# Number biases in Exp and Square, and one full-width product for both float16 halves, in a four-layer graph network

## The chip, the cores and the metric

The kernel runs on one NeuronCore of a Trainium2 chip. The metric is the device time of one execution in microseconds; the time of the kernel before is the median of three runs. The core's engines are named as in the profile: PE (TensorE, matrix products; PEld is its weight load), DVE (VectorE), ACT (ScalarE), POOL (GpSimd) and SP (SyncE, which issues most transfers).

## The reference

Four graph layers work on 4096 nodes with 64 features and one dense 4096 x 4096 adjacency matrix of zeros and ones. After every layer the input is added and a layer norm over the features follows.

```python
# layer 0: mean over neighbours, a linear map, relu, rows scaled to length one
h = (adj @ x + x) / clip(sum(adj, 1) + 1, 1); z = relu(concat([x, h]) @ W + b); z / norm(z)
# layers 1 and 3: attention in hyperbolic space, over all pairs (i, j)
adj_att = sigmoid(left[:, None] + right[None, :] + b_att) * adj
support = einsum('ij,ijd->id', adj_att, logmap(x[:, None], x[None, :]))
proj(expmap(x, support))
# layer 2: the last 100 neighbours of each node, weighted by powers of two
rank = cumsum(adj != 0, axis=1); deg = rank[:, -1:]; k = minimum(deg, 100)
w = mask * where(rank - (deg - k) > 0, 0.5 ** (deg - rank), 0)
w @ (x @ weight) + bias
```

In layer 2 an edge that is the n-th from the end of its row weighs 2 to the power of -n. The weight thus follows from a count of the edges that come after it.

## The kernel before, in words

Nodes are cut in 32 blocks of 128 (the neighbours j, on the partitions) and in four groups of 1024 (the nodes i, along the free axis). Each layer walks the groups in the order 3, 2, 1, 0 (`GROUPS`) and, within a group, the blocks from the last to the first. The adjacency matrix is read anew by every layer, in loads of two blocks by 1024 nodes (1 MB, `load`, six buffers); its values are taken as bfloat16 by reading every other 16-bit word. A check on DVE (`check`, L838) makes sure that the entries are zero or one. Work on rows (layer norm, the preparation of the next layer, turning of sums) is written as generators that wait in two queues; `tick`, called after every block or so, lets them go on. So row work is strewn between the blocks. In layers 0 and 2 the order of PE and ACT is the order of the program (`manual_schedule(engines=FIXED)`); DVE and POOL there, and all engines in layers 1 and 3, are ordered by the scheduler of the framework.

**Layers 1 and 3** (`attend`). For each block of 128 by 1024 pairs, PE makes scores in a PSUM tile `z` (L1059, L1062, L1065: six products of 512 columns), ACT takes a Sigmoid (L1074, bias is a column of `right`) and a Square of the scores (L1077, bias is the column `turn`, which holds one constant), DVE multiplies (L1080), and for two blocks at once adds and multiplies (L1082); PE sums into `acc` (L1037).

**Layer 2.** `count` (L1569) keeps, for each block, the number of later edges in a PSUM tile `z`. It is updated in place from block to block by two products of 512 columns for each 512 nodes: `pass_by` adds the edges of the block that has just been left, `enter` those of the new one. `weights_of` (L1576) makes the weights with an Exp whose bias is the column `at_edge`, which also holds one constant. The rows to be summed are kept as two float16 halves, high and low, side by side in `halves` (128 columns for each block). `add_up` (L1581) sums with four products of 64 columns: high and low half, each for the first and the second 512 nodes, into the two partition halves of one tile `acc`. All four lag one block behind the Exp.

Groups 3 and 2 go together (`wide_pass`, Exp of 1024 columns), then group 1 and group 0 one at a time (`narrow_pass`, Exp of 512 columns). The text calls these the two-group pass and the one-group passes. PSUM holds three tiles `z` of two banks. In layer 2 the third, `third_z`, gives its first half to the sums of the second group of the two-group pass and lends its second half to row work (`of_third`, in turn with `aux`).

At the end of a pass ACT copies the sums to SBUF (L1611), and `end_2` has PE turn them back to rows by four transposes (`to_rows_of`, L1095); DVE scales them and adds the bias (L1494, L1498), and layer norm and `prepare` follow: casts of `y` (L899 to L901), transposes (L943), copies of the turned rows (L947), and two small Ln (L950, L951).

Of the kernel before, what the change touches and what calls it, by code (L numbers as in the profile page):

```python
# [19 lines left out]
P = 128  # L20
N = 4096
D = 64
# [36 lines left out]
def gnn_stack_kernel(  # L59
# [509 lines left out]
    def stream(fits):  # L569

        with ExitStack() as st:
# [208 lines left out]

            two_i = keep.tile([P, P], BF16, name="two_i")
            V.tensor_scalar(two_i, ident, 2.0 * UNIT, None, ALU.mult)
            turn = num(keep, "turn", 1)
            V.memset(turn, ROOT + OFF)


            centre = keep.tile([P, 2, D + 1], F32, name="centre")
# [237 lines left out]
            def attend(layer, s, rate, then):  # L1025

                left_b = left_bs[s]

                acc = ps.tile([P, W], F32, name="acc")
                lag = []  # L1030

                def add_up(g, t, behind=None):

                    for k in (1, 0):
                        j = 2 * g + k
                        for h in range(2):
                            it = nc.tensor.matmul(  # L1037
                                acc[h * D : (h + 1) * D, :], xe[:, j, :],
                                t[:, k, h * W : (h + 1) * W],
                                start=j == BLOCKS[0], stop=j == BLOCKS[-1],  # L1040
                            )
                            if behind is not None:
                                in_order(it.ins, behind.ins)

                for g in reversed(range(NB // 2)):
                    _, edge = load(s, g)
                    need((layer, 2 * g // WB))
                    if g == 4 and then is not None:
                        later(in_turn((layer, then, "left"), spread_left(then)), True)
                    for k in (1, 0):  # L1050
                        j = 2 * g + k
                        of = slice(j * P, (j + 1) * P)

                        zp = z_tile()
                        for h in range(2):
                            half = zp[:, h * W : (h + 1) * W]
                            to = slice(s * WW + h * W, s * WW + (h + 1) * W)
                            at = k * WW + h * W
                            nc.tensor.matmul(  # L1059
                                half, two_i, edge[:, at : at + W], start=True, stop=False  # L1060
                            )
                            nc.tensor.matmul(  # L1062
                                half, hi_lo[:, of], lo_hi[:, to], start=False, stop=False
                            )
                            last = nc.tensor.matmul(  # L1065
                                half, src[:, of], dst[:, to], start=False, stop=True
                            )
                        if k == 1:
                            if len(lag) == 2:
                                add_up(*lag.pop(0), last)  # L1070
                            sq = sb.tile([P, 2, WW], F32, name="sq")
                            t = sb.tile([P, 2, WW], F32, name="t", bufs=3)
                        sig = sb.tile([P, WW], F32, name="sig", bufs=3)
                        nc.scalar.activation(  # L1074
                            sig, left_b, AF.Sigmoid, bias=right[:, j : j + 1]
                        )
                        nc.scalar.activation(  # L1077
                            sq[:, k], zp, AF.Square, bias=turn, scale=-1.0 / UNIT
                        )
                        V.scalar_tensor_tensor(t[:, k], zp, 0.0, sig, ALU.max, ALU.mult)  # L1080
                        tick(rate)
                    V.scalar_tensor_tensor(t, sq, HIGH**2, t, ALU.add, ALU.mult)  # L1082
                    lag.append((g, t))
                    tick(rate)
                for args in lag:
                    add_up(*args)
                sums = row.tile([P, W], F32, name="sums", bufs=2)
                nc.scalar.copy(sums, acc)
                return sums
# [200 lines left out]
            )  # L1290
            V.tensor_sub(enter, enter, edge_of)
            V.tensor_sub(pass_by, pass_by, enter)
            at_edge = num(keep, "at_edge", 1)
            V.memset(at_edge, -(OFF_EDGE + CUT) * LN2)


            w2_twice = keep.tile([P, D], F32, name="w2_twice")
            w2_hl = keep.tile([P, 2, D], F16, name="w2_hl")

# [188 lines left out]
            def end_2(s, sums):  # L1488
                z = grp("z0")
                yield 1  # L1490
                yield from free()
                t = to_rows_of(sums)
                yield 1
                V.scalar_tensor_tensor(  # L1494
                    z.rearrange("p (h k) f -> p h k f", h=2)[:, 0], t[:, 0], 2.0**CUT / SUP,
                    b2_sb[:, None, :].to_broadcast([P, SB, D]), ALU.mult, ALU.add,
                )
                V.scalar_tensor_tensor(  # L1498
                    z.rearrange("p (h k) f -> p h k f", h=2)[:, 1], t[:, 1], 2.0**CUT / SUP,
                    b2_sb[:, None, :].to_broadcast([P, SB, D]), ALU.mult, ALU.add,  # L1500
                )
                held.pop()
                yield 1
                V.tensor_add(z, z, x_of(2)[:, blocks(s), :])
                yield 1
                yield from norm_rows(3, s, z, x2[:, blocks(s)])
                yield from prepare(3, s, att3, batt3_sb, curve3, 1e-30, good[:, 1], 40)

            def wide_pass(two):

                zs = [z_tile() for _ in two]

                accs = [ps.tile([P, W], F32, name="acc"), third_z[:, :W]]
                behind, lag = [None, None], []
                for g in reversed(range(NB // 2)):
                    edges = [load_2(s, g) for s in two]
                    need((2, 2 * g // WB))
                    for k in (1, 0):
                        j = 2 * g + k
                        w = sb.tile([P, 2, WW], F32, name="sq").bitcast(BF16)[:, :, :WW]  # L1520
                        for i, edge in enumerate(edges):
                            here = edge[:, k * WW : (k + 1) * WW]
                            count(zs[i], behind[i], here, j, WW)
                            behind[i] = here
                            weights_of(zs[i], WW, w[:, i])
                            if i == 1:
                                for of, acc in enumerate(accs if lag else ()):
                                    add_up(acc, *lag[of])
                                lag = [(j, w[:, n, :W], w[:, n, W:]) for n in range(2)]
                            if two[0] != GROUPS[0] or j < BLOCKS[4]:  # L1530
                                tick(1)
                for of, acc in enumerate(accs):
                    add_up(acc, *lag[of])
                return accs

            def narrow_pass(s):

                zs = [z_tile() for _ in range(2)]
                acc = ps.tile([P, W], F32, name="acc")
                behind, lag = [None, None], []  # L1540
                for g in reversed(range(NB // 2)):
                    edge = load_2(s, g)
                    for k in (1, 0):
                        j = 2 * g + k
                        w = sb.tile([P, 2, WW], F32, name="sq").bitcast(BF16)[:, 0, :WW]
                        for h in range(2):
                            here = edge[:, k * WW + h * W : k * WW + (h + 1) * W]
                            count(zs[h], behind[h], here, j, W)
                            behind[h] = here
                            weights_of(zs[h], W, w[:, h * W : (h + 1) * W])  # L1550
                        if lag:
                            add_up(acc, *lag.pop(0))
                        lag.append((j, w[:, :W], w[:, W:]))
                        tick(1)
                add_up(acc, *lag.pop(0))
                return [acc]

            def load_2(s, g):
                a, edge = load(s, g)
# [13 lines left out]

            def weights_of(z, n, w):

                weighed[0] = nc.scalar.activation(w, z[:, :n], AF.Exp, bias=at_edge, scale=-LN2)  # L1576

            def add_up(acc, j, *ws):
                for part in range(2):
# [24 lines left out]
            with tc.manual_schedule(engines=FIXED):  # L1604
                spare.append(of_third)

                for some in (GROUPS[:2], GROUPS[2:3], GROUPS[3:]):
                    accs = wide_pass(some) if len(some) == 2 else narrow_pass(some[0])
                    for s, acc in zip(some, accs):
                        sums = row.tile([P, W], F32, name="sums", bufs=2)  # L1610
                        nc.scalar.copy(sums, acc)  # L1611
                        later(end_2(s, sums))
                spare_ends()

# [96 lines left out]
```

## Time and profile before

| | before |
|---|---|
| median of three runs | 1103.39 us (1102.56 to 1103.76) |
| the profiled execution | 1103.6 us |
| its span in the profile | 1101.8 us, mean granted TensorE clock 0.966 |
| PE busy | 997.7 us (91%) |
| DVE busy | 916.4 us (83%) |
| ACT busy | 795.1 us (72%) |
| layer 0, about | 0 to 195 us |
| layer 1, about | 195 to 520 us |
| layer 2, two-group pass | 520 to 629 us |
| layer 2, one-group passes | 629 to 750 us |
| layer 3 and the end | 750 to 1102 us |

The stage borders are read from the first and last starts of the lines named above. A share of busy time is a mean over stages of different kinds; what sets the time of a stage is seen in its own windows and timeline. A matmul's duration in the timeline is longer than the distance between the starts of two that follow each other, since they are pipelined: the distance is what counts.

### The profile page before, as it was taken

The page shows a single profiled execution, that of the slowest core. Times are in us where ns is not written, and L with a number is a line of the kernel's source. Part 1 is how long each engine was busy: PE and PEld are TensorE (multiplying, and loading weights), DVE is VectorE, ACT ScalarE, POOL GpSimd, SP SyncE. Part 2 cuts the span into 40 slices and gives each one's busy share as a digit, 9 for nine tenths or more (in the row PEclk, how much of TensorE's full clock was granted, in tenths as well). Part 3 has the DMA queues.
Part 4 walks back from the last instruction along what each step waited for, and adds up shares of the span by engine and source line. Part 5 has one row for each costly group of instructions (what it writes and reads, how often), then busy time and mean ns, then how long its engine had stood idle before and what let it go on. Part 6 is the DMA issues. An engine that isn't in the chain of part 4 may idle for free.

```text
span 1101.8 us, 13740 instructions
## 1 busy us (share of the span) xinstructions
PE 997.7 (91%) x4862; PEld 394.3 (36%) x4949; DVE 916.4 (83%) x1452; ACT 795.1 (72%) x886; POOL 273.5 (25%) x649
## 2 busy tenths in 40 slices
PE   4998997889999999998998998998899999999980
PEld 2454454333333333332333333322333333333320
DVE  6677976999999999999457395636999999999986
ACT  0003122979999999897676778989899999998950
POOL 0011210010053533625500010100001544346172
PEclk8999998889999999999998999999999999999995
DMA  9999999536666566655787988776556666666400
GB/s 358 378 411 388 369 421 382 189 122 223 214 244 211 195 234 214 222 198 184 271 304 280 366 298 277 273 261 229 191 192 217 241 228 202 238 222 228 163 1 23
DMA packets 38581, 271.63 MB, mean 247 GB/s; under 512 B 4710, under 2 KB 4710, under 8 KB 5734
## 3 DMA queue, kind: packets, MB, share of 16 engines
q1 hardware_dynamic: 37728, 270.03, 67.4%
q8 instruction: 41, 0.67, 0.2%
q10 hardware_dynamic: 774, 0.63, 0.2%
q14 instruction: 38, 0.31, 0.1%
HBM read 269.58 MB, written 1.05 MB: 246 GB/s over the span
## 4 chain that ended last, share of the span: by engine, by line
PE 56%; DVE 26%; ACT 8%; DMA 3%; POOL 3%; issue 3%; ACTq 0%; SPq 0%; POOLq 0%; DVEq 0%
PE acc L1037 15%; PE z L1569 9%; DVE t L1082 8%; PE z L1062 7%; PE z L1059 7%; PE z L1065 6%; DVE t L1080 6%; PE acc L1581 3%; PE acc L1414 3%; ACT sq L1077 3%; DMA edges<-in_adj_dram 3%; DVE junk L838 2%; ACT sq L1576 2%; PE z L1581 1%; POOL sq L869 1%
## 5 line engine op out<-in xcount | busy, mean ns | idle before, releaser
L1080 DVE SCALAR_TENSOR_TENSOR t<-z,sig 128x1024 f32<-128x1024 f32 x256 | 309.3, 1219 | 13.8 <-ACT sq L1077 7.5
L1077 ACT ACTIVATE sq<-z,turn 128x1024 f32<-128x1024 f32 x256 | 277.9, 1111 | 46.5 <-PE z L1065 19.4
L1082 DVE SCALAR_TENSOR_TENSOR t<-sq,t 128x2048 f32<-128x2048 f32 x128 | 297.4, 2324 | 0.5
L1074 ACT ACTIVATE sig<-left_b,right 128x1024 f32<-128x1024 f32 x256 | 286.0, 1146 | 1.9 <-DVE t L1080 1.3
L1037 PE MATMUL acc<-t,xe 128*64 128x512 f32 x1024 | 258.2, 614 | 16.5 <-DVE t L1082 15.7
L1062 PE MATMUL z<-lo_hi,hi_lo 128*128 128x512 f16 x512 | 195.4, 382 | 3.6 <-issue 0.7
L1065 PE MATMUL z<-dst,src 74*128 74x512 f16 x512 | 196.6, 384 | 0.0
L1059 PE MATMUL z<-edges,two_i 128*128 128x512 bf16 x463 | 183.0, 395 | 6.8 <-DVE t L1080 6.8
L1576 ACT ACTIVATE sq<-z,at_edge 128x512 bf16<-128x512 f32 (+1 forms) x192 | 149.2, 828 | 45.2 <-PE z L1569 41.9
L1037 PEld LDWEIGHTS acc<-t,xe 128*64 128x64 f32 x1024 | 64.3, 137 | 145.6 <-issue 85.1
L838 DVE SCALAR_TENSOR_TENSOR t<-edges 128x2048 bf16<-128x2048 f32 x32 | 73.0, 2288 | 37.0 <-DMA edges<-in_adj_dram 37.0
L1059 PEld LDWEIGHTS <-two_i 128*128 128x128 bf16 x512 | 50.5, 99 | 132.7 <-issue 83.9
L1569 PE MATMUL z<-edges,pass_by 128*128 128x512 bf16 x241 | 86.2, 395 | 11.0 <-ACT sq L1576 10.3
L1414 PE MATMUL acc<-edges,first 128*128 128x512 bf16 x241 | 77.0, 396 | 18.4 <-DMA edges<-in_adj_dram 17.9
L1569 PE MATMUL z<-edges,enter 128*128 128x512 bf16 x240 | 84.0, 393 | 0.5
L1414 PE MATMUL acc<-edges,third 128*65 128x512 bf16 x256 | 80.1, 394 | 0.8 <-issue 0.2
L838 DVE SCALAR_TENSOR_TENSOR junk<-edges 128x2048 bf16<-128x2048 f32 x32 | 73.2, 2286 | 4.8 <-DMA edges<-in_adj_dram 4.6
L1065 PEld LDWEIGHTS <-src 74*128 74x128 f16 x512 | 49.4, 97 | 71.0 <-issue 9.1
L1062 PEld LDWEIGHTS <-hi_lo 128*128 128x128 f16 x512 | 50.6, 99 | 54.9 <-issue 10.0
L1581 PE MATMUL acc<-sq,halves 128*64 128x512 bf16 x384 | 61.0, 395 | 2.4 <-issue 1.4
L869 POOL TENSOR_TENSOR sq<-z 128x512 f32<-128x512 f32 x8 | 14.2, 1777 | 166.5 <-DVE z L868 135.1
L1133 POOL TENSOR_TENSOR w_att<-x,u 128x512 f32<-128x512 f32 x6 | 15.6, 2596 | 142.1 <-ACT u L1128 142.1
(375 smaller groups left out, 938.4 us busy)
## 6 DMA issues: line engine op xcount, KB each, us to landing
edges<-in_adj_dram SPq DMA_DIRECT2D x256, 1024.0 KB, 4.9
x<-in_x_dram SPq DMA_DIRECT2D x4, 256.0 KB
out_dram<-x ACTq DMA_DIRECT2D x2, 256.0 KB
out_dram<-x SPq DMA_DIRECT2D x2, 256.0 KB
w_sb<-in_L_gnn_W_dram ACTq DMA_DIRECT2D x1, 32.0 KB, 5.4
w_twice<-in_L_gnn_weight_dram ACTq DMA_DIRECT2D x2, 16.0 KB, 7.4
given<-in_L_gnn_b_dram ACTq DMA_DIRECT2D x1, 0.2 KB
given<-in_L_gnn_bias_dram ACTq DMA_DIRECT2D x1, 0.2 KB
```

The lines of the kernel that those rows point to most:

```text
L838: V.scalar_tensor_tensor(junk, a, 0.0, a, ALU.not_equal, ALU.not_equal, accum_out=odd[:, n : n + 1])
L1037: it = nc.tensor.matmul(acc[h * D : (h + 1) * D, :], xe[:, j, :], t[:, k, h * W : (h + 1) * W], start=j == BLOCKS[0], stop=j == BLOCKS[-1],)
L1059: nc.tensor.matmul(half, two_i, edge[:, at : at + W], start=True, stop=False)
L1062: nc.tensor.matmul(half, hi_lo[:, of], lo_hi[:, to], start=False, stop=False)
L1065: last = nc.tensor.matmul(half, src[:, of], dst[:, to], start=False, stop=True)
L1074: nc.scalar.activation(sig, left_b, AF.Sigmoid, bias=right[:, j : j + 1])
L1077: nc.scalar.activation(sq[:, k], zp, AF.Square, bias=turn, scale=-1.0 / UNIT)
L1080: V.scalar_tensor_tensor(t[:, k], zp, 0.0, sig, ALU.max, ALU.mult)
L1082: V.scalar_tensor_tensor(t, sq, HIGH**2, t, ALU.add, ALU.mult)
L1414: nc.tensor.matmul(accs[h][:m], lhs[:, j, :], edge[:, at : at + W], start=j == BLOCKS[0], stop=j == BLOCKS[-1],)
L1569: nc.tensor.matmul(z[:, h : h + W], lhs, rhs[:, h : h + W], start=j == BLOCKS[0], stop=True, skip_group_check=True,)
L1576: weighed[0] = nc.scalar.activation(w, z[:, :n], AF.Exp, bias=at_edge, scale=-LN2)
```

## The change

The two constant columns `turn` and `at_edge` are gone; Square and Exp get the constants as numbers in the instruction. In the one-group passes the two halves of `halves` are no longer summed apart. One product with all 128 columns is made for each 512 nodes, so that the partitions of a sum hold the high half above and the low half below. There are now two tiles of sums, one for each 512 nodes: `acc` and the first half of `third_z`. Each product comes right behind the counting products of its own 512 nodes and takes the weights of the block before. After the pass both tiles are copied, and the two partition halves are added while the rows are turned back: eight float32 products with `stack`, two identity matrices of 64 above each other. The two-group pass sums as before.

```diff
-            turn = num(keep, "turn", 1)
-            V.memset(turn, ROOT + OFF)
...
-                            sq[:, k], zp, AF.Square, bias=turn, scale=-1.0 / UNIT
+                            sq[:, k], zp, AF.Square, bias=ROOT + OFF, scale=-1.0 / UNIT
...
-            at_edge = num(keep, "at_edge", 1)
-            V.memset(at_edge, -(OFF_EDGE + CUT) * LN2)
+            stack = keep.tile([P, D], F32, name="stack")
+            V.tensor_add(stack, ident[:, :D], ident[:, D:])
...
-                t = to_rows_of(sums)
+                if len(sums) == 1:
+                    t = to_rows_of(sums[0])
+                else:
+                    t = take(F32, P, SB, 2, D)
+                    for k in range(SB):
+                        for h, of in enumerate(sums):
+                            nc.tensor.matmul(
+                                t[:, k, h], of[:, k * P : (k + 1) * P], stack,
+                                start=True, stop=True,
+                            )
+                    t = t.rearrange("p k h f -> p h k f")
...
             def narrow_pass(s):
 
                 zs = [z_tile() for _ in range(2)]
-                acc = ps.tile([P, W], F32, name="acc")
-                behind, lag = [None, None], []
+                accs = [ps.tile([P, W], F32, name="acc"), third_z[:, :W]]
+                behind, lag = [None, None], [None, None]
+
+                def add(h):
+                    if lag[h] is not None:
+                        j, w = lag[h]
+                        nc.tensor.matmul(
+                            accs[h], halves[:, j, :], w,
+                            start=j == BLOCKS[0], stop=j == BLOCKS[-1],
+                        )
+
                 for g in reversed(range(NB // 2)):
...
                             count(zs[h], behind[h], here, j, W)
                             behind[h] = here
-                            weights_of(zs[h], W, w[:, h * W : (h + 1) * W])
-                        if lag:
-                            add_up(acc, *lag.pop(0))
-                        lag.append((j, w[:, :W], w[:, W:]))
+                            add(h)
+                            part = w[:, h * W : (h + 1) * W]
+                            weights_of(zs[h], W, part)
+                            lag[h] = (j, part)
                         tick(1)
-                add_up(acc, *lag.pop(0))
-                return [acc]
+                for h in range(2):
+                    add(h)
+                return [accs]
...
-                weighed[0] = nc.scalar.activation(w, z[:, :n], AF.Exp, bias=at_edge, scale=-LN2)
+                weighed[0] = nc.scalar.activation(w, z[:, :n], AF.Exp, bias=-(OFF_EDGE + CUT) * LN2, scale=-LN2)
...
-                    for s, acc in zip(some, accs):
-                        sums = row.tile([P, W], F32, name="sums", bufs=2)
-                        nc.scalar.copy(sums, acc)
+                    for s, of in zip(some, accs):
+                        sums = [row.tile([P, W], F32, name="sums", bufs=2) for _ in of]
+                        for to, acc in zip(sums, of):
+                            nc.scalar.copy(to, acc)
                         later(end_2(s, sums))
```

## The prediction

> **What bounds the kernel now.** I read the page first (engine totals, then the chain that ended last), then the sums of two windows, one for each one-group pass of layer 2, then the groups kept apart by shape, and last the timelines of PE and ACT inside a one-group pass.
>
> ```profile
> span 1101.8 us, 13740 instructions
> PE 56%; DVE 26%; ACT 8%; DMA 3%; POOL 3%; issue 3%; ACTq 0%; SPq 0%; POOLq 0%; DVEq 0%
> 628.80:688.80 60.00, 53.93 (x305) 18.52 (x310) 43.30 (x141) 49.34 (x79) 6.59 (x16) 1.00 0.85 298
> 688.80:749.20 60.40, 55.20 (x328) 18.97 (x332) 28.58 (x84) 52.26 (x83) 4.74 (x8) 0.97 0.78 267
> ```
>
> More than half of the chain is PE. The two lower rows are the one-group passes (length, then busy time of PE, PEld, DVE, ACT, POOL, granted clock, DMA share, GB/s): 60 us each for 32 blocks, PE busy for 90%, the clock at 0.97 to 1.00. Transfers do not set the time here: no PE wait for an edge load stands in these windows.
>
> ```profile
> L1077 ACT ACTIVATE sq<-z,turn 128x1024 f32<-128x1024 f32 x256 | 277.9, 1111 | 46.5 <-PE z L1065 19.4 <-DVE t L1082 14.6 <-DVE r_t L754 3.0
> L1576 ACT ACTIVATE sq<-z,at_edge 128x512 bf16<-128x512 f32 x128 | 81.3, 687 | 17.8 <-PE z L1569 17.7
> L1439 ACT COPY top<-acc 128x512 f32<-128x512 f32 x8 | 4.7, 588 | 24.3 <-PE acc L1414 24.3
> L899 ACT CAST ys<-y 128x512 f16<-128x512 f32 x8 | 4.9, 618 | 39.6 <-DVE y L896 39.6
> L1134 ACT ACTIVATE sq<-u 128x512 f32<-128x512 f32 x6 | 3.8, 628 | 0.0
> L1239 PE MATMUL aux<-w_sb,x_t 64*128 64x64 f32 x64 | 8.8, 278 | 0.0
> ```
>
> Behind the first bar stand the busy time in us and the mean of one in ns, behind the second the idle time before them. Square and Exp read PSUM and a bias column; the Square of L1134 reads SBUF and has no bias column.
>
> ```profile
> 640.00 0.39 PE L1569 MATMUL z<-edges,pass_by 128*128 128x512 bf16 x1
> ...
> 640.22 0.39 PE L1569 MATMUL z<-edges,enter 128*128 128x512 bf16 x1
> ...
> 640.45 0.39 PE L1569 MATMUL z<-edges,pass_by 128*128 128x512 bf16 x1
> ...
> 640.67 0.39 PE L1569 MATMUL z<-edges,enter 128*128 128x512 bf16 x1
> 640.71 1.26 ACT L1576 ACTIVATE sq<-z,at_edge 128x512 bf16<-128x512 f32 x2 [0.78 <-PE z L1569]
> ...
> 640.99 0.62 PE L1581 MATMUL acc<-sq,halves 128*64 128x512 bf16 x4
> ...
> 641.55 0.40 PE L1569 MATMUL z<-edges,pass_by 128*128 128x512 bf16 x1
> ...
> 649.19 0.62 ACT L899 CAST ys<-y 128x512 f16<-128x512 f32 x1 [0.67 <-DVE y L896]
> ...
> 650.75 1.25 ACT L1576 ACTIVATE sq<-z,at_edge 128x512 bf16<-128x512 f32 x2
> ...
> 651.48 0.39 PE L1569 MATMUL z<-edges,pass_by 128*128 128x512 bf16 x1 [1.75 <-ACT sq L1576]
> ```
>
> Each row begins with its start and its length in us. Down to 641.55 it is one block of a one-group pass: four counting products 0.2225 us apart, the two Exp begun under them, four half-width sums, and the next block 1.55 us after the first. The last three rows show the other regime: row work on ACT waits for DVE, Exp comes late, PE stands 1.75 us.
>
> **The full-width product (one-group passes).** Now a block costs PE 1.55 to 1.57: counts to the first sum 0.99, the four sums 0.56. Two halves of 64 columns run side by side, since four start within 0.56 where four full-width ones would take 0.90. So the change does not remove two of four products' streaming: two pairs become two singles, 0.45. What goes is the rest: 0.11 inside the sums and 0.10 ahead of them (0.32 from the last count to the first sum, instead of 0.22). Six full-width products at 0.2225 make 1.335.
>
> Whether PE can run that fast hangs on ACT, because each count tile is updated in place: the next count of a tile waits for its Exp. The loop of one tile: second product starts 0.22 after the first, ends 0.39 later, Exp starts 0.10 later (640.61 to 640.71), lasts 0.687, and PE follows 0.04 to 0.06 after it (650.75 + 0.687 to 651.48): 1.44 us. With a shorter Exp (below) it is 1.35. So I take 1.37 a block, 0.195 less than now; 64 blocks make 12.5 us.
>
> Taken off: in the first such pass PE's lead does not help before the cast at 649.19, since that cast already waits 0.67 for a DVE row chain that has been busy since 631.9; 14 blocks x 0.195 = 2.7 are handed back there as a longer wait. Twelve copies of turned rows (L947, 1.0 us on ACT) stand between Exp pairs; a pair of blocks with one takes 3.6 now and, by the loop above with 0.9 of copy in it, about 3.33 after, so 0.13 short of the full saving each: 1.6. Left: 8.2.
>
> **What it adds.** The sums of a one-group pass come as two tiles. A second ACT copy (L1439's shape, 0.59, overlapped to 0.5) stands before the next pass's first Exp: 0.5 on the path. Turning them back is eight float32 products against `stack` instead of four transposes. The nearest row is L1239, 8.8 us for 64 records, two for each product: 0.275 each, 2.2 against 0.65 now: 1.55 more of PE, on the path for group 1 (turned in the second one-group pass). For group 0 it falls into the start of layer 3, where PE waits for DVE anyway and DVE itself now waits 2.3 for these rows; the order of the two programs puts the two copies ahead of the first Sigmoid (1.0 later) and the turning one score tile earlier (sooner by more than that). I count zero, bounds -2 to +2. `stack` is one DVE add of 64 columns at the start, and two one-column memsets go: nothing. The odd half of the sums now goes into the first half of `third_z`, whose second half is lent to row work; the price of that is a rival.
>
> **Biases as numbers.** No row shows the same activation with and without the column. L1134 against the cast L899 prices a function over a copy at 0.01 (628 and 618, both SBUF). A PSUM copy of 512 is 588, so an Exp without a column should be near 598 against 687: 0.09 less. Bounds 0 and 0.10; I take 0.09, as both shapes agree. In layer 2's two-group pass a pair of blocks' worth of PE (2.90 in the timeline) covers Exp, and only stalls behind row work gain: 6.9 us of Exp are on the chain there, six pieces x 0.09 = 0.6.
>
> In layers 1 and 3 a step of two blocks takes 4.66 to 4.69, and DVE (2 x 1219 + 2324, less small overlaps) and PE (12 x 0.22 + 1.94 of L1037) both fill it; ACT, at about 4.2, does not. So 256 x 0.09 = 23 us of ACT are mostly covered. They count where ACT is behind after row work:
>
> ```profile
> DVE t L1080 <- ACT sq L1077: 7.5, 17, 0.8
> ```
>
> That bounds it above at some 7.5. From below: Square holds 28 us of the chain, 25 pieces x 0.09 = 2.3. I take 3. The two score layers are not ordered by hand, and the order of the two programs does change there (Sigmoid and Square swap places by one or two, mostly at group ends); no instruction is added. Today's steps at such places are 3.45 to 6.19 around the mean of 4.67, so a dozen changed places may give or take 4 us together; I count zero and put it in the range.
>
> **Sum.** 8.2 - 1.55 - 0.5 + 0.6 + 3.0 = 9.7 us. The profiled execution took 1103.6 (1.8 of it outside the span), 0.2 above the median of three: 1093.9 against it, 1093.7 against the median.
>
> **Rivals.** First, no difference: the 0.21 that I see around the half-width sums belongs to the change of operands, not of width, and stays. Then a block stays at 1.56, the sums still cost two slots, and 3.6 of ACT gain less 2.05 of additions leaves 1.6: 1101.8. For it: the halves do run in pairs. Against: in layer 1 the score products follow each other 0.22 apart across three changes of operand. The Trainium skill ("TensorE: Matmul & The Clock Gate", Part 3: Packing small matmuls) says that products in different column groups run at once, about 4 ns apart; by it alone the change saves no streaming, and the trace agrees with that (0.56, not 0.90). The Trainium skill ("TensorEngine Tiling (Array Packing)", Key Properties) also says that a change of tiling mode drains the engine; by that the 0.10 and 0.11 would go, as I forecast.
>
> Second, a small gain: the bias as a number shortens nothing. The loop of 1.44 then binds, 0.12 a block, 64 x 0.12 = 7.7; less 1.7 for the hidden blocks, 1.6 for copies and 2.05 added: 2.35, so 1101.0.
>
> Third, slower: false waits on `third_z`. In the order of the changed program the sum into its first half waits nine times for an ACT copy out of the second half, and twice for DVE's reading of turned rows. A copy is 1.0; DVE may have a 2.29 check (L838) and row work ahead, about 5. If all lie open, 9 + 10 = 19; against 9.7 that is 9 slower, 1112; half-open copies and full DVE waits give 14.5, so 1108.2. It decides from 0.9 a wait on. Against it: PE's next count waits for an Exp queued behind the same copy anyway, and DVE's wait of group 2 falls into the stretch already lost before 649.19.
>
> A fourth, larger gain: all 64 blocks at 1.34 and all ACT waits of layers 1 and 3 gone, 14.4 + 7.5 + 0.6 - 2.05 = 20.5, 1082.9.
>
> **The numbers.** Forecast (gain 6 to 14) 0.52, larger 0.10, small gain 0.16, no difference 0.09, slower 0.13. A measurement of this kernel tells about 0.2%, 2.2 us, from no change; so faster 0.78, same 0.09, slower 0.13. The range 1084 to 1102 leaves out the end of the large gain, the slower case and part of no difference.
>
> **What would show it.** Right: one-group passes near 56 us with blocks 1.35 to 1.40 apart, six products evenly 0.22 apart; Exp of 512 near 0.60 and Square near 1.02; steps of layers 1 and 3 still 4.66. Wrong: Exp unchanged (then blocks near 1.44); blocks still 1.55; PE waiting for ACT copies or DVE ahead of a sum into `third_z`; or layers 1 and 3 longer by more than 4 us, which would be the new order.

## The result, and the profile after

The changed kernel takes 1093.36 us, the median of 6 runs (1089.49 to 1095.15), against 1103.04 for the kernel before, the median of 6 (1099.21 to 1105.3): a ratio of 0.9908 [0.9884, 0.9932], 9.7 us faster. Run again beside the experiments, it took 1094.14 (8 runs), a ratio of 0.9929 [0.9899, 0.996]. The forecast was 1093.7.

The first lines of its page, the span and the chain that ended last by engine:

```profile
span 1087.7 us, 13618 instructions
PE 62%; DVE 24%; ACT 6%; POOL 2%; DMA 2%; issue 2%; ACTq 0%; SPq 0%; POOLq 0%; DVEq 0%
```

PE holds more of the chain than before (62%, it was 56%). The profiled run, 1089.49, is the fastest of its six, and 5.0 of the 14.1 us between the two spans lie in layer 0, which the change does not touch: over the 14 profiles of this study layer 0 takes 189.9 to 195.9 us whatever the kernel. So stages are compared here, cut at the first Square or Exp of each (the last two blocks of layer 3 are counted with the end):

| us | layer 1 | two-group pass | one-group passes | start of layer 3 | layer 3 | end |
|---|---|---|---|---|---|---|
| before | 325.3 | 108.3 | 60.1 + 60.9 | 4.5 | 308.1 | 39.5 |
| after | 321.3 | 106.8 | 59.5 + 57.0 | 4.9 | 307.0 | 41.0 |
| after, run again | 321.5 | 107.9 | 59.6 + 57.0 | 4.9 | 307.0 | 40.7 |

Without layer 0 that is 9.1 us, 8.0 in the second profile. The groups that the prediction named, kept apart by shape:

```profile
L1075 ACT ACTIVATE sq<-z 128x1024 f32<-128x1024 f32 x256 | 254.7, 1021 | 57.8 <-PE z L1063 25.6 <-DVE t L1080 21.1 <-DVE r_t L754 3.5
L1594 ACT ACTIVATE sq<-z 128x512 bf16<-128x512 f32 x128 | 74.4, 600 | 19.3 <-PE z L1587 18.4
L1553 PE MATMUL acc<-sq,halves 128*128 128x512 bf16 x64 | 25.0, 391 | 0.3 <-ACT sq L1594 0.3
L1553 PE MATMUL z<-sq,halves 128*128 128x512 bf16 x64 | 24.9, 389 | 2.9 <-DVE z L1506 1.4 <-ACT lo_hi L945 0.5 <-ACT dst L945 0.4
L1496 PE MATMUL aux<-stack,sums 128*128 128x64 f32 x16 | 2.2, 281 | 0.7 <-ACT sums L1630 0.7
L1437 ACT COPY top<-acc 128x512 f32<-128x512 f32 x8 | 4.7, 587 | 20.6 <-PE acc L1412 20.5
```

Square fell from 1111 to 1021 ns, the Exp of 512 from 687 to 600, while the copy, which never had a bias, stayed at 588 and 587: a bias as a number is worth 87 to 90 ns. The Trainium skill ("ScalarE: Activation LUTs", What ACT_TABLE_LOAD costs) gives 93 ns for each operand of that kind; the trace is close. The 128 full-width products replace 256 of half width. One block of a one-group pass in the timeline (start, length; of all engines only PE and ACT are shown, here and in the timelines below):

```profile
621.18 0.38 PE L1553 MATMUL acc<-sq,halves 128*128 128x512 bf16 x1
621.40 0.39 PE L1587 MATMUL z<-edges,pass_by 128*128 128x512 bf16 x1
621.44 1.20 ACT L1594 ACTIVATE sq<-z 128x512 bf16<-128x512 f32 x2 [0.57 <-PE z L1587]
621.63 0.39 PE L1587 MATMUL z<-edges,enter 128*128 128x512 bf16 x1
621.85 0.38 PE L1553 MATMUL z<-sq,halves 128*128 128x512 bf16 x1
622.09 0.39 PE L1587 MATMUL z<-edges,pass_by 128*128 128x512 bf16 x1
622.32 0.39 PE L1587 MATMUL z<-edges,enter 128*128 128x512 bf16 x1
622.54 0.38 PE L1553 MATMUL acc<-sq,halves 128*128 128x512 bf16 x1
```

From one sum into `acc` to the next it is 1.36 us, six products 0.22 to 0.24 apart. That was forecast at 1.37. Yet the passes are 59.5 and 57.0 long, not near 56. The windows of the two passes (length, busy times of PE, PEld, DVE, ACT, POOL, then granted clock, DMA share, GB/s), and below them three of 3.41 us in the first pass:

```profile
618.30:677.80 59.50, 51.14 (x246) 23.05 (x246) 43.03 (x141) 46.60 (x81) 6.60 (x16) 0.94 0.83 299
677.80:734.80 57.00, 51.27 (x285) 24.61 (x285) 28.80 (x84) 49.34 (x84) 4.75 (x8) 0.97 0.82 287
636.69:640.10 3.41, 1.30 (x6) 0.48 (x5) 3.41 (x8) 2.26 (x5) 3.15 (x6) 1.00 0.95 375
640.10:643.51 3.41, 3.11 (x8) 1.15 (x8) 3.41 (x12) 1.93 (x4) 0.99 (x3) 0.51 0.46 192
643.51:646.92 3.41, 3.41 (x23) 1.69 (x21) 3.38 (x27) 2.39 (x4) 0.00 (x0) 0.99 0.47 127
```

The granted clock is 0.94 and 0.97, where it was 1.00 and 0.97 before. In the window from 640.10 it is one half, and PE got through 8 products instead of 23. The timeline there:

```profile
640.40 0.59 PE L1587 MATMUL z<-edges,pass_by 128*128 128x512 bf16 x1 [2.42 <-ACT sq L1594]
640.78 0.63 PE L1587 MATMUL z<-edges,enter 128*128 128x512 bf16 x1
641.21 0.63 PE L1553 MATMUL acc<-sq,halves 128*128 128x512 bf16 x1
...
641.63 0.63 PE L1587 MATMUL z<-edges,pass_by 128*128 128x512 bf16 x1
```

PE stood 2.42 us for an Exp that is queued behind casts that wait for DVE, and then products are 0.43 apart. The same follows the two stalls of 2.52 us at which ACT loads the tables for Ln and back (664.0 and 705.0). By the distances of Exp pairs, against those of the filled kernel below, each of the three windows costs 1.45 to 1.6 us, 4.6 together. The kernel before has stalls of 1.75, 2.45 and 2.46 us in its passes and one such window.

### The profile page after: what moved, and what is told of

Its sections match the earlier page's. It is cut to its first block, busy times and chain, and to the rows that moved or that the text cites. A ratio compares the mean times of both kernels' runs of the same rounds, so it can differ in the third digit from the quotient of the medians.

```text
span 1087.7 us, 13618 instructions
## 1 busy us (share of the span) xinstructions
PE 996.7 (92%) x4845; PEld 404.7 (37%) x4845; DVE 913.4 (84%) x1451; ACT 761.7 (70%) x888; POOL 265.0 (24%) x649
## 4 chain that ended last, share of the span: by engine, by line
PE 62%; DVE 24%; ACT 6%; POOL 2%; DMA 2%; issue 2%; ACTq 0%; SPq 0%; POOLq 0%; DVEq 0%
PE acc L1035 17%; PE z L1587 9%; PE z L1057 8%; PE z L1063 7%; PE z L1060 7%; DVE t L1080 6%; DVE t L1078 6%; PE acc L1412 4%; DVE junk L836 3%; ACT sq L1594 2%; DMA edges<-in_adj_dram 2%; PE acc L1599 2%; ACT sq L1075 1%; PE z L1599 1%; PE aux L941 1%
## 5 line engine op out<-in xcount | busy, mean ns | idle before, releaser
L1078 DVE SCALAR_TENSOR_TENSOR t<-z,sig 128x1024 f32<-128x1024 f32 x256 | 309.9, 1220 | 13.9 <-ACT sq L1075 11.8
L1080 DVE SCALAR_TENSOR_TENSOR t<-sq,t 128x2048 f32<-128x2048 f32 x128 | 295.3, 2307 | 0.2
L1075 ACT ACTIVATE sq<-z 128x1024 f32<-128x1024 f32 x256 | 254.7, 1021 | 57.8 <-PE z L1063 25.6
L1057 PE MATMUL z<-edges,two_i 128*128 128x512 bf16 x512 | 202.5, 395 | 6.3 <-DVE t L1078 6.3
L1594 ACT ACTIVATE sq<-z 128x512 bf16<-128x512 f32 (+1 forms) x192 | 136.7, 740 | 51.2 <-PE z L1587 48.0
L1587 PE MATMUL z<-edges,pass_by 128*128 128x512 bf16 x248 | 89.1, 400 | 11.3 <-ACT sq L1594 10.9
L1412 PE MATMUL acc<-edges,first 128*128 128x512 bf16 x256 | 82.9, 406 | 14.3 <-DMA edges<-in_adj_dram 14.2
L1587 PE MATMUL z<-edges,enter 128*128 128x512 bf16 x256 | 91.2, 399 | 0.0
L1412 PE MATMUL acc<-edges,third 128*65 128x512 bf16 x256 | 82.3, 404 | 0.0
L1060 PEld LDWEIGHTS <-hi_lo 128*128 128x128 f16 x512 | 50.4, 99 | 62.9 <-issue 17.4
L1131 POOL TENSOR_TENSOR w_att<-x,u 128x512 f32<-128x512 f32 x6 | 12.7, 2123 | 147.8 <-ACT u L1126 147.8
L1412 PEld LDWEIGHTS <-third 128*65 128x65 bf16 x256 | 29.3, 114 | 34.4 <-issue 5.4
```

The costliest lines, as they stand in the source:

```text
L1057: nc.tensor.matmul(half, two_i, edge[:, at : at + W], start=True, stop=False)
L1060: nc.tensor.matmul(half, hi_lo[:, of], lo_hi[:, to], start=False, stop=False)
L1075: nc.scalar.activation(sq[:, k], zp, AF.Square, bias=ROOT + OFF, scale=-1.0 / UNIT)
L1412: nc.tensor.matmul(accs[h][:m], lhs[:, j, :], edge[:, at : at + W], start=j == BLOCKS[0], stop=j == BLOCKS[-1],)
L1587: nc.tensor.matmul(z[:, h : h + W], lhs, rhs[:, h : h + W], start=j == BLOCKS[0], stop=True, skip_group_check=True,)
```

## The experiments

Each kernel was timed beside the kernel before: 1101.71 (median of 25 runs) for both biases, full width, Square alone and the changed kernel once more; 1102.18 (20) for Exp alone, Exp as a column, the filled kernel and the later casts; 1101.94 (11) for the other four.

### One part at a time: both numbers, the full-width product, Square's number, all of it again

```diff
 both biases only: the kernel before, with
-   AF.Square, bias=turn, ...          +   AF.Square, bias=ROOT + OFF, ...
-   AF.Exp, bias=at_edge, ...          +   AF.Exp, bias=-(OFF_EDGE + CUT) * LN2, ...
 full width only: narrow_pass, end_2 and stack of the changed kernel; both columns kept
 Square only: the kernel before, with the first of the two lines
```

Both biases:

> The kernel before with both biases as numbers, sums of layer 2 unchanged. Prediction's own accounting: 3.6 us faster (3.0 in layers 1 and 3, 0.6 in the two-group pass), nothing in the one-group passes, where PE sets the block at 1.56. Theory after seeing the changed kernel's trace: the second L1080 of a step of two blocks waited some 0.1 us for the first Square in nearly every step; with Square 0.09 shorter the step goes from 4.66 to 4.58, so some 100 undisturbed steps bring 7 us, less what the new order takes; together 5 to 8 us faster, steps of 4.58, blocks of the one-group passes still 1.56.

Full width:

> The kernel before with the full-width product alone; both bias columns stay. By the loop of count and Exp (1.44 us with the Exp of 0.687) blocks of the one-group passes come 1.44 apart, not 1.36; 0.12 x 64 = 7.7 less 1.7, 1.6 and 2.05 as in the prediction: 2.4 us faster. If the half-clock stretches of PE after long stalls (seen three times in the one-group passes of the changed kernel, once before, about 1.6 us each) come from the faster blocks, they come here too and leave 0 to 2 us slower or the same. Rival (no hand-over between Exp and count binds): blocks 1.34 to 1.36, 6 us faster. Steps of layers 1 and 3 stay 4.66.

Square:

> The kernel before with the number as bias in Square alone. Theory: all of the gain in layers 1 and 3 is Square's, steps of 4.58: 4.5 to 7 us faster, within 1 us of both biases together. Rival (prediction): only where ACT is behind, 3 us, steps of 4.66.

The changed kernel once more:

> The changed kernel again, beside the parts on the same chip. If the two parts add up, its gain is that of the biases alone plus that of the full width alone plus about 0.08 x 64 less the hidden blocks (some 3 us), because only the shorter Exp lets the block go from 1.44 to 1.36; 9 to 10 us faster in all.

Measured: both biases 1093.25, 0.9932 [0.9908, 0.9955]; full width 1098.31, 0.998 [0.9955, 1.0004]; Square alone 1100.28, 0.9997 [0.998, 1.0014]; the whole change 1094.14, 0.9929 [0.9899, 0.996]. So the two numbers alone give as much as everything, and the full-width product seems to add nothing to them. Parts do not add up, and two of the three intervals reach 1. The theory ahead of Square alone, 4.5 to 7 us and within 1 us of both numbers together, was missed; so were the 5 to 8 us ahead of both numbers (8.5) and the 9 to 10 ahead of the whole change (7.6).

The profiles say what the medians hide. Without layer 0 Square alone is 3.5 us shorter than the kernel before, Exp alone (below) 3.4 and both numbers 7.0, so these two parts do add up. Typical blocks of the one-group passes, with the two later runs on Exp in their places:

| block, us | Exp's bias a column | Exp's bias a number |
|---|---|---|
| half-width sums | 1.56 (before) | 1.56 (both biases; Exp only) |
| full-width sums | 1.45 (full width only; Exp as column) | 1.36 (changed) |

A block with both numbers and half-width sums:

```profile
627.95 0.40 PE L1565 MATMUL z<-edges,pass_by 128*128 128x512 bf16 x1
...
628.67 1.09 ACT L1572 ACTIVATE sq<-z 128x512 bf16<-128x512 f32 x2 [0.48 <-PE z L1565]
628.96 0.62 PE L1577 MATMUL acc<-sq,halves 128*64 128x512 bf16 x4
629.51 0.40 PE L1565 MATMUL z<-edges,pass_by 128*128 128x512 bf16 x1
```

ACT stands 0.48 us there and waits for PE. So each half of the change needs the other: at half width PE sets the block, whatever Exp takes, and at full width the loop of one count tile through Exp does. Full width alone came out at 1.45, as the theory had it (1.44), not at the 1.34 to 1.36 of its rival. That the two numbers win as much in the end is the clock: their passes have one half-clock window, the changed kernel's three.

### Exp's number alone, and Exp's column in the changed kernel

```diff
 Exp only: the kernel before, with the line of Exp above, and Square's column kept
 Exp as column: the changed kernel, with
-   AF.Exp, bias=-(OFF_EDGE + CUT) * LN2, ...
+   AF.Exp, bias=at_edge, ...
```

Exp's number alone:

> The kernel before with only Exp's bias as a number. Theory (a shorter Exp also shortens the stalls of TensorE in layer 2, and fewer windows run at half clock): the two stalls of 2.45 and 2.46 us in the one-group passes come to about 2.3, blocks stay at 1.56, 3 to 5 us faster than before. Rival (the prediction's accounting: without the full-width product Exp's gain counts only in the two-group pass): 0.6 us faster, that is, no difference that can be measured.

Exp as a column:

> The changed kernel with Exp's bias as a column again (Square's stays a number). Theory (the loop of one count tile through Exp sets the block): blocks of the one-group passes 1.45 instead of 1.36, 64 of them less those hidden, 4 to 5 us slower than the changed kernel at the same granted clock. Rival (TensorE's six products set the block): blocks 1.36, within 1 us of the changed kernel.

Exp's number alone took 1098.66, 0.9966 [0.9946, 0.9985], 3.5 us faster with blocks still at 1.56: the theory held, and the prediction's accounting (0.6) fell. Both passes together came from 121.0 to 117.8, each of the two kernels with one half-clock window in them: where ACT is late after row work, a shorter Exp counts at half width too, and the Ln stalls came from 2.46 to 2.30.

Exp as a column in the changed kernel:

```profile
623.46 1.29 ACT L1596 ACTIVATE sq<-z,at_edge 128x512 bf16<-128x512 f32 x2 [0.15 <-PE z L1589]
623.65 0.39 PE L1589 MATMUL z<-edges,enter 128*128 128x512 bf16 x1
623.87 0.38 PE L1555 MATMUL z<-sq,halves 128*128 128x512 bf16 x1
624.20 0.39 PE L1589 MATMUL z<-edges,pass_by 128*128 128x512 bf16 x1
...
624.91 1.29 ACT L1596 ACTIVATE sq<-z,at_edge 128x512 bf16<-128x512 f32 x2 [0.15 <-PE z L1589]
```

Exp pairs are 1.45 apart, and PE starts a count 0.33 after a sum where 0.22 is its pace: the loop is seen directly. By the medians this kernel is only 0.7 us behind the changed one (1094.82, 0.9943 [0.9921, 0.9964]), but its runs had a mean granted clock of 0.9703 against 0.9661. A line through all 153 runs of this study (a constant for each kernel, one slope for the clock: 0.63 us for each 0.001 of it) puts it some 5 us behind at the same clock, where 4 to 5 were expected. The line leaves 1.6 us of scatter and is a description, no proof; the next run tests the clock's part directly.

### Filling the stalls

```diff
+            no_weight = keep.tile([P, P], BF16, name="no_weight")
+            V.memset(no_weight, 0.0)
...
+                fills = {13: 8, 25: 8} if s == GROUPS[2] else {15: 8}
...
+                        for _ in range(fills.get(block, 0)):
+                            nc.tensor.matmul(
+                                accs[0], no_weight, behind[1], start=False, stop=False,
+                            )
```

> The changed kernel with eight more products of zero weights (they add nothing to the sums) put into TensorE's queue ahead of each of the three stalls of 2.4 to 2.5 us in the one-group passes. No other engine's order changes. Theory (the granted clock is halved for a window of 3.41 us when TensorE was busy for less than about 45% of the window before): the stalls come to about 0.7 us, the half-clock windows at 640, 664 and 705 us go, mean granted clock about 0.004 higher, and the two passes together are 3 to 4.5 us shorter although TensorE has 24 products more. Rival (the clock follows something else): the windows stay, and the kernel is the same or up to 1 us slower.

It took 1088.78, 0.987 [0.9845, 0.9895], 5.4 us faster than the changed kernel beside the first four. The two passes:

```profile
621.30:677.70 56.40, 51.70 (x263) 23.79 (x262) 43.07 (x141) 46.57 (x80) 7.32 (x16) 1.00 0.84 317
677.70:733.60 55.90, 51.52 (x292) 24.92 (x292) 28.46 (x84) 49.36 (x83) 2.76 (x8) 1.00 0.80 292
```

and the place of the stall of 2.42 us:

```profile
641.30 1.52 PE L1568 MATMUL acc<-edges,no_weight 128*128 128x512 bf16 x6
...
643.43 0.39 PE L1596 MATMUL z<-edges,pass_by 128*128 128x512 bf16 x1 [0.62 <-ACT sq L1603]
643.66 0.39 PE L1596 MATMUL z<-edges,enter 128*128 128x512 bf16 x1
643.88 0.38 PE L1557 MATMUL acc<-sq,halves 128*128 128x512 bf16 x1
```

The clock stays at 1.00, the stall is 0.62, products behind it are 0.22 apart, and the passes are 112.3 together, 4.2 shorter, although PE does 24 products more. The order of ACT's and of PE's other instructions is the same; the framework moved some of DVE's row work. That the halved clock follows the stall and costs about this much is shown. The passes are now 56.4 and 55.9, near the 56 that was forecast.

The trace allows one step further. Its record of the clock changes on a grid of 3.413 us. In the 14 profiles, between 50 and 1050 us, a window at full clock with PE busy for less than 45% was followed by one at half clock in 72 of 73 cases; at 45 to 55% in 6 of 43; above that in 9 of 3867. So a stall of 2.5 us does it or not by where it falls. The share is a description and not the whole rule: three of the last nine, all in layer 0, follow windows in which PE was busy throughout. The kernel before shows both, two stalls of the same length:

```profile
670.82:674.23 3.41, 1.82 (x15) 0.69 (x15) 3.14 (x12) 3.36 (x6) 0.00 (x0) 1.00 0.87 288
674.23:677.64 3.41, 2.38 (x12) 0.73 (x11) 3.34 (x25) 2.81 (x5) 0.00 (x0) 1.00 0.56 238
677.64:681.05 3.41, 3.41 (x18) 0.89 (x16) 2.98 (x8) 2.79 (x5) 0.00 (x0) 1.00 0.67 204
715.19:718.60 3.41, 1.06 (x4) 0.29 (x3) 3.41 (x16) 3.20 (x6) 0.00 (x0) 1.00 0.92 308
718.60:722.01 3.41, 3.41 (x13) 0.79 (x12) 3.21 (x19) 2.03 (x4) 0.00 (x0) 0.51 0.01 2
```

The stall that ends at 675.3 is cut by a border (PE busy 53% and 70%) and nothing follows; the one that ends at 717.5 lies in one window (31%), and the next has 0.51. The Trainium skill ("TensorE: Matmul & The Clock Gate", Part 1: The HAM clock gate) describes a free-running window of 3413 ns, as seen here, but has the clock fall after an idle window of some 3.4 us. Here 2.1 us of standing within one window was enough (636.69 to 640.10 above: PE busy for 1.30 of 3.41).

### Both biases, half width, with the stalls filled

```diff
 both biases only (above), with no_weight and fills as in the filled kernel, into acc
```

> The kernel before with both biases as numbers, half-width sums kept, and the eight zero-weight products ahead of each of the three long stalls as in the filled version of the changed kernel. Theory (the full-width product is worth about 3.9 us at an equal granted clock, and the changed kernel lost that to half-clock windows): no half-clock window in either pass, and 2.5 to 4.5 us slower than the filled changed kernel (1088.8), so 1091 to 1093. Rival (full width is worth nothing once the biases are numbers): within 1 us of 1088.8.

It took 1092.11, 0.9922 [0.9904, 0.9941], with the clock at 1.00 in both passes:

```profile
622.10:681.00 58.90, 57.79 (x327) 19.82 (x326) 42.95 (x141) 43.84 (x80) 6.61 (x16) 1.00 0.86 303
681.00:738.40 57.40, 55.49 (x342) 19.39 (x340) 28.81 (x85) 46.88 (x84) 4.85 (x8) 1.00 0.84 285
```

They are 116.3 together. With full width it is 112.3 and 1088.78. So the full-width product is worth 3.3 us in the medians and 4.0 in the passes once no window is at half clock; without the filling the same step is worth nothing (1093.25 to 1094.14). This is where that gain went.

### The casts one block later

```diff
-                yield from prepare(3, s, att3, batt3_sb, curve3, 1e-30, good[:, 1], 40)
+                yield from prepare(3, s, att3, batt3_sb, curve3, 1e-30, good[:, 1], 42)
```

> The changed kernel with the casts of the row work that turns layer 2's sums into layer 3's rows one block later, so that the cast of the first one-group pass finds its DVE rows nearer to ready. Theory: TensorE's stall of 2.42 us at 640 us comes to about 1.2, no half-clock window follows it, the first one-group pass is 1.5 to 2.8 us shorter than in the changed kernel; the stalls at 664 and 705 stay with their windows. Rival (the row chain only ends later by as much): same as the changed kernel within 0.5 us.

It took 1089.48, 0.9879 [0.9856, 0.9903], more than was expected. The stall became 1.15 and no window at half clock follows; the first pass is 54.7 long, the second 56.1. But the stalls at Ln, still 2.52, were not followed by one either in this profile, which is luck of the grid worth some 3 us, and layer 3 with its start is 1.4 longer, with a stall of 4.36 at 746.8. What the later cast alone is worth is not separated from that luck here.

### Without lending `third_z`

```diff
+                    if len(some) == 1:
+                        spare.clear()
                     accs = wide_pass(some) if len(some) == 2 else narrow_pass(some[0])
```

> The changed kernel, but in the one-group passes the second half of third_z is not lent to row work; all row work goes through the other PSUM tile. This tests the prediction's third rival. Theory (the waits of sums for third_z, 2.9 us in the trace, mostly stand where TensorE would wait for an Exp anyway): the waits ahead of sums go, and the time stays within 1 us of the changed kernel. Rival (they cost what they show): 2.5 to 3 us faster than the changed kernel.

The waits of the sums for `third_z` went from 2.9 us to 0.2, but PE's stall behind the first cast grew from 2.42 to 3.90:

```profile
645.58 0.39 PE L1587 MATMUL z<-edges,pass_by 128*128 128x512 bf16 x1 [3.90 <-ACT sq L1594]
```

The 1.35 us that PE had waited for DVE at 631.9 came back there, since the cast waits for the same chain. The passes are 115.9 together instead of 116.6 in the second profile of the changed kernel: mostly hidden in this execution, as the theory has it. The medians say more: 1088.51, 0.9872 [0.9856, 0.9889], which is 5.6 below the changed kernel and more than the theory or its rival allowed. The profiled run, 1093.05, is the slowest of its five, so no trace shows one of the faster ones; at the same clock the line through all runs leaves some 2 us. What the false waits cost stays open: 0.7 us by the passes, 2 by the line, 5.6 by the medians.

### Filling the two-group pass too

```diff
+                    if g == WB // 2 - 1:
+                        for _ in range(9):
+                            nc.tensor.matmul(
+                                accs[0], no_weight, behind[1][:, :W], start=False, stop=False,
+                            )
                     need((2, 2 * g // WB))
 the second of the two kernels: also the casts one block later, with fills = {26: 8} and {16: 8}
```

With the casts where they are:

> The filled changed kernel with nine more zero-weight products ahead of the stall of 2.7 us in the two-group pass, where TensorE waits for the last group's supports (592 us). Theory: the two half-clock windows behind it (6.8 us) go and the two-group pass is 2 to 3 us shorter, so about 1086. Rival (the second stall of 1.1 us behind the first still leaves a window below 45%, or the supports come later): same as the filled kernel.

With later casts:

> The same as the run before it, with the casts one block later and the zero-weight products moved to the stalls that are left (two instead of three). Theory: the first one-group pass 1.5 us shorter than with the casts where they are, layer 3's start 1 to 2 us longer (in the run with late casts TensorE stood 4.4 us there): within 1.5 us of the run before, either way. Rival (layer 3's start is covered by the next group's work): 1.5 to 2 us faster than the run before.

The first took 1084.54 (1084.14 to 1086.2), 0.9841 [0.9827, 0.9855]; the second 1086.53, 0.9854 [0.9834, 0.9874], with the first pass 1.8 shorter and layer 3 with its start 1.4 longer, as expected. Two runs of the second took 1082.3 and 1082.8 and three 1086.5 to 1087.6, and without layer 0 both profiles are 890.5 long, so which of the two is faster is not settled. Two windows of the same place, of the kernel that fills only the one-group passes and then of the first of these two:

```profile
588.50:592.50 4.00, 1.20 (x14) 0.54 (x10) 2.19 (x2) 1.32 (x3) 1.89 (x1) 1.00 0.43 180
592.50:599.30 6.80, 5.82 (x32) 2.39 (x32) 0.69 (x1) 3.55 (x4) 0.00 (x0) 0.50 0.45 157
```

```profile
588.50:592.50 4.00, 3.50 (x19) 1.15 (x17) 2.98 (x4) 2.02 (x3) 1.88 (x1) 1.00 0.68 285
592.50:599.30 6.80, 5.66 (x48) 2.66 (x48) 0.69 (x1) 4.03 (x5) 0.00 (x0) 1.00 0.41 136
```

Two windows at half clock are gone, the two-group pass is 105.3 instead of 108.0. By its median the first of these kernels is the fastest of the study: 8.8 us below the changed kernel's first median, 17.4 below the kernel before. Filling and not lending were not tried together.

## Why the prediction was right, point by point

**The one-group passes** (8.2, less 1.55 and 0.5: 6.15 forecast). The block was right: 1.36 for 1.37, and the table of blocks shows that it is bound on both sides as the prediction had it, six products on PE and the loop through Exp. The rival of the small gain had the right loop, 1.45 for its 1.44, but a bias as a number does shorten Exp. The first rival, that the 0.21 around the half-width sums stays, is out: products are evenly spaced, and the Trainium skill's sentence on the drain at a change of tiling mode ("TensorEngine Tiling (Array Packing)", Key Properties) agrees with the 0.21 that went. The weight loads show where it stood: in the kernel before, PE loads the weights of a count 0.22 us ahead, while the product before it runs, but those of the first half-width sum (640.99) and of the first count behind the sums (641.54) only as their products start; in the undisturbed blocks of the changed kernel all are loaded 0.22 ahead. The width and the place of the sums were changed together and not tried apart. Measured, the passes gained only 4.5 (121.0 to 116.5). The step that failed is that stalls behind row work were carried over at their length and the granted clock of 0.97 to 1.00 with them. Shorter blocks left the stalls at 2.4 to 2.5 us, one of them longer by 0.67, and the windows at half clock went from one to three. With the stalls filled the gain is 8.7; of that some 1.5 is the window of the kernel before, so 7.2 stands against 6.15. Pairs of blocks with a copy of turned rows took 3.35 to 3.53, where 3.33 was forecast.

**Handed back before the cast** (2.7). Mis-sized: PE's stall there grew from 1.75 to 2.42, with 1.35 of new waiting for DVE ahead of it: 2.0, before the clock's share. PE stalls there ahead of the 14th block, so 13 blocks, not 14, come before it.

**The fold and the second copy** (1.55 and 0.5). The fold's 16 matrix records take 2.2 us for one group and 1.9 for the other, against 2.2 assumed; neither term was isolated by a run. For group 0 zero was counted; the start of layer 3 is 0.5 longer (4.45 to 4.95), in full width alone too, and not with both numbers.

**Exp in the two-group pass** (0.6). 108.3 to 106.8 and 107.9 in two profiles of the same kernel; the half-clock windows behind its stall of 2.67 us move it by more than the term.

**Square** (3.0, bounds 2.3 to 7.5). The size was near: with Square alone layer 1 is 4.3 shorter, layer 3 0.2 shorter and the end 1.3 longer, 3.2 in all; the medians show 1.4 and the ratio 0.3, with an interval that includes none. The reason was wrong. The wait that bounded the term grew instead of shrinking:

```profile
DVE t L1078 <- ACT sq L1075: 11.8, 23, 0.9
```

It was 7.5 us in 17 waits. What shrank are 69 waits of 0.15 us or less of a DVE product right behind a Square, too short for that list: 6.3 us together before, 2.1 in 64 after. All waits of these products together are as long as before (13.8 us, 13.9 after, 12.9 with Square alone), so they hold little of the gain. A part of it stands in DVE's add and multiply on two blocks, here before and after:

```profile
L1082 DVE SCALAR_TENSOR_TENSOR t<-sq,t 128x2048 f32<-128x2048 f32 x128 | 297.4, 2324 | 0.5
L1080 DVE SCALAR_TENSOR_TENSOR t<-sq,t 128x2048 f32<-128x2048 f32 x128 | 295.3, 2307 | 0.2
```

It takes 2306 or 2307 ns in every kernel with Square's number and 2323 to 2331 in every one with the column, 2.1 us less over 128 of them; why, no run shows. The steps of layers 1 and 3 did not stay at 4.66, as the prediction said they would: their median went from 4.69 to 4.62 in layer 1 and from 4.67 to 4.60 in layer 3, and longer waits took back about what the short ones gave. That the changed order of the two programs made them is argued and not shown, since no run kept the old order with the shorter Square.

**The rival on the other side**, false waits on `third_z` at 1108.2. They are there, 2.9 us instead of 14, in the row of L1553 above, and their largest, 1.35, falls into the stretch already lost, as was argued against it. What they cost stays open, as said under the kernel without lending.

**The larger gain** (1082.9) needed blocks of 1.34 and no waits behind Square left; neither came.

So the total, 9.7 forecast and 9.7 measured (7.6 when run again), holds to within what the clock's windows move; that the first medians meet it to 0.1 us is luck. The passes fell 1.6 short through the windows, the layers with Square came to 3.2 by the stages of the first table, where 3.0 was forecast, and the two-group pass gave 0.9 more in one profile and 0.2 less in the other.

## What to carry to other kernels

Read an in-order loop from both sides before shortening one of them: here the cheaper product alone was worth 0.11 us a block, the cheaper activation alone nothing in an undisturbed block, and both together 0.20. When a change makes PE's bursts shorter, look at each stall of about 2 us or more for the granted clock of the window behind it, since that can take back more than the stall itself. Harmless products ahead of such a stall are cheap, provided they end before PE is wanted.

## What the hardware showed that was not expected

The clock halves after far less than a whole window of idling: below 45% of PE busy time in a window of 3.413 us, 72 times in 73, and by stalls of 2.3 to 2.7 us that lie well in one window. Each such window cost 1.45 to 1.6 us in the one-group passes of the changed kernel. The mean granted clock goes with about half of the run-to-run variance of this kernel: over 56 runs of the kernel before, 1096.56 to 1109.72, time and clock correlate with -0.72. Products with all-zero weights kept the clock up here (24 of them, 1.00 in both passes).
